# A decoder layer in fp32 on one core: a second pair of blocks by two levels, a longer preparation in the attention stages, and loads in another order

## The chip, the core and the metric

The kernel runs on one core of a Trainium2 chip. The core has engines that run their own instruction queues side by side: TensorE (PE in the profile; its weight loads are shown apart as PEld), VectorE (DVE), ScalarE (ACT), GpSimd (POOL) and SyncE (SP). DMA transfers are issued by an engine's queue and run beside all of them. The metric is the device time of one execution, in microseconds (us). Before the change it is 2240.34 us, the median of three runs (2240.03 to 2240.9).

## The reference

One decoder layer in fp32, for x of 16 batches x 128 rows x 1024 columns and a context of the same shape:

```python
x = x + attention(layernorm(x), Wqkv, bqkv, Wo, bo)       # one head of 256 columns
x = x + cross(layernorm(x), ctx, ctx, Wq, Wk, Wv, Wo, bo, g)
x = x + feed_forward(layernorm(x), gate, up, down)

def cross(q, k, v, Wq, Wk, Wv, Wo, bo, g):   # "linear" attention over 128 channels, 8 heads of 64
    qh, kh, vh = heads(q Wq), heads(k Wk), heads(v Wv)
    qh = softmax(qh, axis=head_dim) * SCALE
    kh = softmax(kh, axis=columns)
    context = einsum('bhdn,bhen->bhde', kh, vh)
    out = einsum('bhde,bhdn->bhen', context, qh) Wo + bo
    norm = maximum(sqrt(sum(out * out, axis=channels)), 1e-12)
    return out / norm * g * sqrt(128)

def feed_forward(x, gate, up, down):         # 1024 -> 2752 -> 1024
    Wg, Wu, Wd = dequantize(gate), dequantize(up), dequantize(down)
    # each: two int4 nibbles per int32, (nibble - zero) * scale in groups of 64
    return (silu(x Wg) * (x Wu)) Wd
```

## The kernel before

**Stages.** The program goes through five stages, one after the other:

1. Self-attention, four tiles of four batches (0 to 250 us of the profiled execution).
2. Cross-attention, one batch after the other (250 to 758 us). A batch takes four *key units* and four *query units*: a key unit is `kq <- wk_sb, cx` on TensorE, an exponential on ScalarE (`ek <- kq`, L727) and `kx <- ek, cxt` on TensorE; a query unit is `kq <- wq_sb, xn`, an exponential (`qe <- kq`, L795), a sum and reciprocal on VectorE, a multiplication on GpSimd (`qe`, L806), a transpose on VectorE, and a store and a load through DRAM (`kd`, then `qs`), after which `mm <- qs, m_sb` and the norm of the result follow, in `project_out`. The norm's root is Ln and Exp (L877, L878).
3. The gate and up projections of the feed-forward, pass 0: the tokens of batches 8 to 15 (758 to 1298 us).
4. The same, pass 1: the tokens of batches 0 to 7 (1298 to 1760 us).
5. The down projection (1760 to 2239 us).

**Multiplying by fewer products.** The 2752 rows of the feed-forward are cut into ten blocks of 256 and a last one of 192 (`RB = 10`). For a block by *one level*, a two by two split of weights and tokens is computed with seven products in place of eight (`one_block`; its products are the seven names of `GATE`). For a pair of blocks by *two levels* the seven are split once more, which makes 49 smaller products (`two_levels`, L1188 on: outer products `OUTERS`, in each of them seven inner ones). The combinations of inputs and results that this needs are made on VectorE and GpSimd: `ti` from the tokens, `li` from the weights, `C` and other sums from the results. Pass 1 works on all five pairs by two levels. In pass 0, `PAIRS = [3]` says which pairs are done so: blocks 6 and 7, the rest by one level, in the order 0 to 5, the pair, 8, 9, and the last block (`last_block`).

**Preparing the weights.** The weights are dequantised and combined for their seven products by `prepare` (a generator; each `next` is one *step*). A job is a block's matrix: "g", "u" or "d" (gate, up, down; "r" and "m" for the last block's gate and up). A job has two dequantising steps on VectorE (each two nibble operations and two multiplications or subtractions) and one step of four combinations; its seven results go to DRAM by seven stores of 256 KB. Raw weights are loaded on SyncE's queue, one or two units ahead. Before, `EARLY = 5` blocks' gate and up (ten jobs, thirty steps) are prepared in stage 1, with stores on GpSimd's queue, and the rest in stage 3, `rest`, with gate, up and down of each block in turn, and stores on SyncE's queue.

**What sets the order.** In stages 2 to 5 TensorE, VectorE and SyncE run in the program's order, through the wrappers `tensor`, `vector` and `sync` (class `InOrder`). All that goes through them is recorded at one line, L63, so the tiles' names tell it apart. The order of stage 2 is written out by hand: `later(n, fn)` puts `fn` into a list and `tick()`, called after each key unit and each query unit (eight ticks a batch), runs what has come due. At the end of stage 2 the ticks go on between the products of the first feed-forward block (`beside`), until the list is empty; `attention_done` then closes the pools of the cross-attention and opens those of the feed-forward. Self-attention's output projection for its last four batches (`give_half`, matmuls with `wo_again`) is queued so at the first ticks of the cross-attention.

**Loads at the stages' heads.** At the head of stage 2 SyncE's queue gets, in this order: `wk`, `wq`, `wv`, `xwo`, `xbo`, `gs`, then `cx` and `cxt` of the first two batches, then the two halves of `wo_again`. At the head of stage 3, four tiles of weights (`AHEAD = 4`) are loaded: the first on GpSimd's queue, the others on SyncE's; and the tokens' operands (`block_loads(0)`) come in eight loads on SyncE, two ticks apart. The loads of pass 1's tokens (`block_loads(1)`) are put beside every third product after the pair.

**The flag.** The softmaxes of the cross-attention are taken without subtracting the maximum (`plain`). `note` adds each sum and its reciprocal to two running totals on GpSimd (L659); at the end `raise_flag` compares these with `LIMIT` (1e18), counts the rows within it by a matmul with `ones` (`mm <- within`), and if any row is outside, a second copy of the whole program runs, with the maximum subtracted. In the executions here the second copy does not run. Before, one table of activation functions that has Ln and Exp both is loaded once ahead of the cross-attention (`preload_act_table_set`, L672).

Of the kernel before, what the change touches and what calls it, by code (L numbers as in the profile page):

```python
# [18 lines left out]
P = 128  # L19
# [47 lines left out]
def decoder_layer(  # L67
# [95 lines left out]
    def prep_pools(stack, name, c, ahead):  # L163
        for key, bufs in (("a", 3), ("c", c), ("raw", ahead + 1), ("sz", ahead + 1)):
            pools[key] = stack.enter_context(
                tc.tile_pool(name=f"{name}_{key}", bufs=bufs, side="right", reuse_waits="tile")
            )
# [4 lines left out]
    def load_raw(blk, mat, s):  # L172
# [3 lines left out]
        if mat == "d":  # L176
            raw, sz = raw[:w], pools["sz"].tile([P, 2, 512], F32, name="szd")[:w]
            nc.sync.dma_start(raw, dq[ds(start // 2, w), ts(s, 512)])
            for g in range(w // 32):
                row = dsz[start // GROUP + g, ts(s, 1024)].rearrange("(t f) -> t f", t=2)  # L180
                nc.sync.dma_start(sz[ts(g, 32)], row.partition_broadcast(32))
            return raw, *(sz[:, t].unsqueeze(1).to_broadcast([w, 2, 512]) for t in range(2))
# [12 lines left out]
        for m, off, w in parts:  # L195
            q, szs = matrices[m]
            nc.sync.dma_start(raw[:, :, ds(at, w)], q[:, :, ds(off, w)])
            nc.sync.dma_start(
# [6 lines left out]
    def prepare(jobs, ahead, queue, vector=nc.vector):  # L205
# [3 lines left out]
        loads = deque(load_raw(*u) for u in units[:ahead])  # L209
# [6 lines left out]
        for k, (blk, mat, s) in enumerate(units):  # L216
# [6 lines left out]
            if k + ahead < len(units):  # L223
                loads.append(load_raw(*units[k + ahead]))
# [61 lines left out]
    EARLY = 5  # L286

    def give_half(b, h, oT, wo_d, psum, tensor=nc.tensor, vector=nc.vector):
# [19 lines left out]
    prep_pools(first, "q", 4, 1)  # L308
    early = prepare(
        [(blk, mat) for blk in range(EARLY) for mat in "gu"], 1, nc.gpsimd, InOrder(tc, nc.vector)  # L310
    )
    give_pool = ExitStack()
    ag = give_pool.enter_context(tc.tile_pool(name="a_g", bufs=1, reuse_waits="tile"))
    with (
# [166 lines left out]
        for t in range(NT):  # L481
# [38 lines left out]
            else:  # L520

                for i in range(1, BPT):
                    give((t - 1) * BPT + i - 1, oT)
                    value(i, xnT, v)
                atT = turn_weights(at)
# [25 lines left out]
    def block_loads(p, blocks):  # L551

        for n, half in ((0, 0), (1, 0), (1, 1), (0, 1)):
            for i in range(2):
                src = xt_all[p][ds(half * BPT + 2 * i, 2), :, :, :, n]
                tc.keep_in_program_order(
                    nc.sync.dma_start(
# [44 lines left out]
    bcx = unit_pool("b_cx", 2)  # L602
    bw = unit_pool("b_w", 1)
    b0 = unit_pool("b_0", 2)
    bek = unit_pool("b_ek", 3)
    bas = unit_pool("b_as", 1)
    b3 = unit_pool("b_3", 3)
# [4 lines left out]
    bqs = side_pool("b_qs", 5)  # L612
    b1 = side_pool("b_1", 1)
    b2 = side_pool("b_2", 2)
    bps = side_pool("b_ps", 3, space=PSUM)

# [15 lines left out]
    if True:  # L632
        wq_sb = bw.tile([P, HIDDEN], F32, name="wq_sb")
# [7 lines left out]
        sync.dma_start(wk_sb, xwk)  # L641
        sync.dma_start(wq_sb, xwq)
        sync.dma_start(wv_sb, xwv.rearrange("(r p) s -> p r s", p=P))
        sync.dma_start(xwo_sb, xwo.rearrange("(r p) o -> p r o", p=P))
        sync.dma_start(xbo_sb, xbo)
        sync.dma_start(gs_sb, xg)
        vector.tensor_scalar(gs_sb, gs_sb, math.sqrt(S), None, ALU.mult)
        vector.memset(ones, 1.0)
        if plain:

            totals = [bs.tile([P, 2 * HEADS], F32, name=f"total{n}") for n in range(2)]
            for t in totals:
                nc.gpsimd.memset(t, 0.0)

        def note(*both):
            if plain:
                for t, v in zip(totals, both):
                    t = t[:, : v.shape[1]]
                    nc.gpsimd.tensor_tensor(t, t, v, ALU.add)  # L659

        def raise_flag():

            within = [small.tile([P, 1], F32, name=f"within{n}") for n in range(2)]
            for w, t in zip(within, totals):
                vector.tensor_reduce(w, t, AX.X, ALU.add)
                vector.tensor_scalar(w, w, LIMIT, None, ALU.is_le)
            vector.tensor_tensor(within[0], within[0], within[1], ALU.mult)
            ps = bps.tile([P, 1], F32, name="mm")
            tensor.matmul(ps, ones, within[0], start=True, stop=True)
            vector.tensor_copy(flag, ps[0:1])  # L670

        tc.keep_in_program_order(nc.scalar.preload_act_table_set("natural_log_exp_and_others"))  # L672
# [17 lines left out]
        def load_ctx(b):  # L690
            c = bcx.tile([P, C], F32, name="cx")
            sync.dma_start(c, cx[b])
            ct = bct.tile([P, NB, S], F32, name="cxt")
            sync.dma_start(ct, cxt[b])
            return c, ct

        def key_shift(c_sb):

            shift = bas.tile([P, 4, P], F32, name="kshift")
            for oc in range(4):  # L700
# [5 lines left out]
                nmax = small.tile([P, 1], F32, name="knmax")  # L706
# [4 lines left out]
        def key_unit(ctx, p, st):  # L711
# [17 lines left out]
            def use():  # L729
# [16 lines left out]
                if p == 3:  # L746
# [4 lines left out]
                    later(2, lambda: mix(st))  # L751
# [3 lines left out]
        def mix(st):  # L755
# [7 lines left out]
            ksum, krec = (small.tile([P, 4], F32, name=name) for name in ("ksum", "krec"))  # L763
            vector.tensor_copy(ksum, ks)
            vector.reciprocal(krec, ksum)
            note(ksum, krec)
# [17 lines left out]
        def query_unit(xn, pair, qs, wait):  # L784
# [3 lines left out]
            for i in range(2):  # L788
                tensor.matmul(
                    ps[:, i, :], xn[:, ts(2 * pair + i, P)], wq_sb, start=True, stop=True  # L790
# [5 lines left out]
            else:  # L796
                mx = small.tile([P, 2 * HEADS], F32, name="qmx")
# [4 lines left out]
            def weigh():  # L802
                den, rec = (small.tile([P, 2 * HEADS], F32, name=n) for n in ("qden", "qrec"))
# [3 lines left out]
                note(den, rec)  # L807
# [24 lines left out]
        def turned(b):  # L832
# [9 lines left out]
            if b == B - 1:  # L842
                blocks.update(new_blocks(xlate, lambda k: f"X{HB + 2 * k}"))
                loads = block_loads(0, blocks)
                for n in range(8):
                    later(7 + 2 * n, lambda: next(loads))
# [75 lines left out]


        batches = [p + i for p in PASSES for i in range(HB)]
        ctxs = {b: load_ctx(b) for b in batches[:2]}
        wo_again = []
        for d in range(2):
            wo_again.append(bqs.tile([P, C], F32, name="wo_again", tag="qs"))
# [972 lines left out]
```

## Time and profile before

The profiled execution took 2241.3 us; its span, from its first instruction to its last, is 2239.5 us. The table gives, for each stage of the profiled execution, its length, each engine's busy time in it, and the share of time in which the DMA engines were busy:

| stage (us of the span) | length | PE | DVE | ACT | POOL | DMA share |
|---|---|---|---|---|---|---|
| self-attention, 0 to 250 | 250 | 239.6 | 194.0 | 36.4 | 100.6 | 0.47 |
| cross-attention, 250 to 758 | 508 | 502.1 | 339.5 | 243.4 | 208.4 | 0.62 |
| its end, 758 to 850 (with block 0) | 92 | 86.7 | 53.7 | 31.4 | 15.2 | 0.73 |
| pass 0, blocks to 5, 850 to 1074 | 224 | 222.1 | 151.3 | 27.9 | 6.3 | 0.82 |
| pass 0, blocks 6 and 7 by two levels, 1074 to 1163 | 89 | 85.7 | 75.0 | 15.7 | 35.2 | 0.50 |
| pass 0, blocks 8 and 9, 1163 to 1260 | 97 | 97.0 | 61.9 | 12.8 | 0.0 | 0.97 |
| pass 0, last block, 1260 to 1298 | 38 | 38.0 | 23.5 | 4.7 | 6.5 | 0.55 |
| pass 1, all pairs by two levels, 1298 to 1722 | 424 | 423.3 | 323.8 | 82.7 | 181.0 | 0.49 |
| pass 1, last block, 1722 to 1760 | 38 | 38.0 | 17.1 | 5.3 | 0.0 | 0.95 |
| down projection, 1760 to 2239 | 479 | 472.0 | 242.6 | 8.7 | 0.0 | 0.48 |

The page's slices, 56 us each, show the granted TensorE clock and each engine's share, in tenths:

```profile
PE   8999899999999999999999999999999999999998
DVE  6997466667667657666796658787787645544462
ACT  2111135454554431111111112121121000000000
PEclk9999999999999999999999999999999999999999
```

How to read it: PE near its whole length in every stage means that TensorE has work nearly all the time. A wait of TensorE shows as a difference between length and PE. The other engines have room in every stage, though not the same room.

### The profile page before, as it was taken

The page shows a single profiled execution, that of the slowest core. Times are in us where ns is not written, and L with a number is a line of the kernel's source. Part 1 is how long each engine was busy: PE and PEld are TensorE (multiplying, and loading weights), DVE is VectorE, ACT ScalarE, POOL GpSimd, SP SyncE. Part 2 cuts the span into 40 slices and gives each one's busy share as a digit, 9 for nine tenths or more (in the row PEclk, how much of TensorE's full clock was granted, in tenths as well). Part 3 has the DMA queues.
Part 4 walks back from the last instruction along what each step waited for, and adds up shares of the span by engine and source line. Part 5 has one row for each costly group of instructions (what it writes and reads, how often), then busy time and mean ns, then how long its engine had stood idle before and what let it go on. Part 6 is the DMA issues. An engine that isn't in the chain of part 4 may idle for free.

```text
span 2239.5 us, 24114 instructions
## 1 busy us (share of the span) xinstructions
PE 2204.4 (98%) x8330; PEld 1517.3 (68%) x8330; DVE 1482.2 (66%) x2055; ACT 468.9 (21%) x651; POOL 553.1 (25%) x543
## 2 busy tenths in 40 slices
PE   8999899999999999999999999999999999999998
PEld 7556555555555544444774488888887688888887
DVE  6997466667667657666796658787787645544462
ACT  2111135454554431111111112121121000000000
POOL 5452044444444400001320044444442000000000
PEclk9999999999999999999999999999999999999999
DMA  6435246666686768887649834454554964333731
GB/s 251 157 130 169 85 132 198 209 205 197 208 258 192 225 182 287 284 267 253 199 166 301 251 100 158 167 197 155 175 198 165 350 211 164 114 125 129 226 118 39
DMA packets 270835, 425.23 MB, mean 190 GB/s; under 512 B 28784, under 2 KB 130544, under 8 KB 270576
## 3 DMA queue, kind: packets, MB, share of 16 engines
q1 hardware_dynamic: 244624, 377.72, 52.5%
q0 software_dynamic: 8064, 27.27, 3.3%
q10 hardware_dynamic: 18016, 18.62, 2.7%
q8 instruction: 68, 1.11, 0.2%
q14 instruction: 63, 0.52, 0.1%
HBM read 265.62 MB, written 157.35 MB: 189 GB/s over the span
## 4 chain that ended last, share of the span: by engine, by line
PE 90%; DVE 6%; issue 2%; DMA 1%; POOL 1%; ACT 0%; SPq 0%; DVEq 0%; POOLq 0%; ACTq 0%
PE po L1780 21%; PE q L63 20%; PE p L63 18%; PE kq L63 9%; PE mm L63 8%; PE kx L63 5%; PE mm L396 4%; PE mm L411 2%; DVE pa L63 2%; PE p L1157 1%; PE mm L292 1%; PE tr L343 1%; DVE ti L63 1%; DMA wo_again<-in_wo 0%; POOL qe L806 0%
## 5 line engine op out<-in xcount | busy, mean ns | idle before, releaser
L63 PE MATMUL p<-b,w 128*128 128x512 f32 x560 | 248.2, 596 | 1.9 <-DVE sg L63 1.9
L63 PE MATMUL q<-ti,li 128*128 128x256 f32 x1008 | 232.2, 379 | 3.5 <-DVE ti L63 2.8
L63 POOL TENSOR_TENSOR li<-w 128x512 f32<-128x512 f32 x84 | 118.1, 1408 | 433.3 <-DMA w<-wu 244.8
L63 PEld LDWEIGHTS q<-ti,li 128*128 128x128 f32 x1008 | 191.0, 190 | 31.3 <-issue 2.8
L63 PEld LDWEIGHTS p<-b,w 128*128 128x128 f32 x560 | 106.9, 191 | 136.4 <-issue 128.8
L1780 PE MATMUL po<-wc,lc 128*128 128x256 f32 x840 | 183.4, 379 | 0.0
L63 PE MATMUL p<-T,w 128*128 128x512 f32 x400 | 177.2, 592 | 0.0
L1780 PEld LDWEIGHTS po<-wc,lc 128*128 128x128 f32 x840 | 159.6, 190 | 21.8
L63 ACT COPY k<-q 128x512 f32<-128x512 f32 x126 | 73.7, 585 | 399.2 <-PE q L63 399.2
L63 PEld LDWEIGHTS p<-T,w 128*128 128x128 f32 x400 | 76.0, 190 | 95.7 <-issue 95.2
L1780 PE MATMUL po<-wq,lq 128*128 128x256 f32 x560 | 126.7, 379 | 0.2 <-issue 0.2
L806 POOL TENSOR_TENSOR qe<-qe,qrec 128x1024 f32<-128x1024 f32 x64 | 122.0, 1906 | 11.5 <-DVE qrec L63 9.3
L63 PEld LDWEIGHTS mm<-qs,m_sb 128*128 128x128 f32 x512 | 97.3, 190 | 40.1 <-issue 26.8
L63 PE MATMUL kq<-wk_sb,cx 128*128 128x512 f32 x256 | 120.4, 592 | 2.5 <-DMA cx<-in_cx 2.5
L63 PE MATMUL kx<-ek,cxt 128*128 128x512 f32 x256 | 121.8, 598 | 0.0
L63 PE MATMUL mm<-qs,m_sb 128*128 128x256 f32 x512 | 120.8, 379 | 0.0
L63 PE MATMUL kq<-wq_sb,xn 128*128 128x512 f32 x256 | 120.3, 593 | 0.0
L1780 PEld LDWEIGHTS po<-wq,lq 128*128 128x128 f32 x560 | 106.0, 190 | 15.8 <-issue 0.8
L63 DVE TENSOR_TENSOR pa<-pa,sz 128x1024 f32<-128x1024 int32 x86 | 112.6, 1309 | 2.5
L396 PE MATMUL mm<-xnT,wqkv_sb 128*128 128x512 f32 (+1 forms) x320 | 112.9, 509 | 0.0
L63 DVE STREAM_TRANSPOSE kt<-qe 128x1024 f32<-128x1024 f32 x64 | 79.5, 1242 | 43.7 <-POOL qe L806 43.5
L727 ACT ACTIVATE ek<-kq 128x1024 f32<-128x1024 f32 x64 | 65.3, 1020 | 147.4 <-PE kq L63 147.4
(201 smaller groups left out, 3595.7 us busy)
## 6 DMA issues: line engine op xcount, KB each, us to landing
w<-wu SPq DMA_DIRECT2D x140, 256.0 KB, 3.6
lq<-h SPq DMA_DIRECT2D x140, 256.0 KB, 4.4
w<-wg SPq DMA_DIRECT2D x138, 256.0 KB, 2.8
kd<-kt SPq DMA_DIRECT2D x64, 512.0 KB, 2.9
qs<-kd SPq DMA_DIRECT2D x256, 128.0 KB, 3.2
h<-hc SPq DMA_DIRECT2D x80, 256.0 KB, 2.8
wq<-wd SPq DMA_DIRECT2D x70, 256.0 KB, 5.3
h<-h SPq DMA_DIRECT2D x60, 256.0 KB, 3.0
```

Source lines behind the costliest of these rows:

```text
L63: return lambda *args, **kw: self._tc.keep_in_program_order(fn(*args, **kw))
L292: tensor.matmul(ps, oT[:, d, ts(b % BPT, S)], wo_d[d][:, ts(h, 512)], start=(d == 0), stop=(d == 1),)
L343: nc.tensor.transpose(tr[:, j, :], xn[:, ts(4 * h + j, P)], ident)
L396: nc.tensor.matmul(ps[:, tokens], wqkv_sb[:, f, c, :], xnT[:, c, tokens], start=(c == 0), stop=(c == CC - 1),)
L411: nc.tensor.matmul(ps, xnT[:, c, ts(i, S)], wqkv_sb[:, 4:6, c, :], start=(c == 0), stop=(c == CC - 1),)
L727: nc.scalar.activation(ek, ps, AF.Exp)
L806: nc.gpsimd.tensor_tensor(qe, qe, rec.unsqueeze(2).to_broadcast(wide), ALU.mult)
L1157: tensor.matmul(ps, wt[:, j, :], T[q][:, :, j], start=(first == q and j == 0), stop=(q in (2, 3, 4) and j == JC - 1), skip_group_check=True,)
L1780: nc.tensor.matmul(bank[:, i, :], l[:, ts(i, S)], w,  start=(start and c == 0 and i % 2 == 0), stop=(stop and c == len(pairs) - 1), skip_g ...
```

## The change

- **Pairs.** `PAIRS = [3, 4]`: in pass 0 blocks 8 and 9 are also done by two levels, right after blocks 6 and 7. `ti` gets a third buffer, and the operands for the outer product after q = 7 are made beside the second outer product before it. The operands of the last block (`outer_operand`) are made at other products of it.
- **Preparation.** One list `todo` holds all jobs: gate and up of blocks 0 to 9, then "r" and "m", then all "d". Stage 1 does 11 jobs (`EARLY`), three steps more than before, one after each value unit of its last tile. The three next (`MIDDLE = 14`), nine steps, are done in the cross-attention, one at the fifth tick of each of nine batches, with raw loads on `sync` and stores on GpSimd's queue. In block 0 `rest` has a step at the last product alone; its steps per product change in `beside`, and `attention_done` first runs what is left of `middle`. `pools["a"]` has 3 buffers before, 2 or 3 now; `pools["c"]` 4.
- **Head of the cross-attention.** SyncE's queue now gets `wk`, `cx` and `cxt` of the first batch, `wo_again`, then `wq`, `wv`, `xwo`, `xbo`, `gs`, then the second batch. `mix_weights` comes four ticks later, `give_half` two ticks later; the pools are made in another order, and small tiles get a pool of their own (`bsm`).
- **The flag.** `note` and its totals are gone. The sums themselves are kept in a tile of 1088 columns, whose maximum and minimum `raise_flag` takes at the end; the counting matmul comes four ticks after. The load of the activation table ahead of the cross-attention is gone too.
- **Feed-forward's head and pass 1's tokens.** All four first weight tiles go on GpSimd's queue; `block_loads(0)` goes on ScalarE's queue, three ticks apart; `block_loads(1)` is issued all at once after the two-level stage.
- **Ticks.** `mix` two ticks later; `project_out` one tick later for batches up to the thirteenth; the operand for q = 5 one batch later.

The diff, cut to its core:

```diff
+    todo = [(blk, mat) for blk in range(RB) for mat in "gu"] + [(RB, "r"), (RB, "m")]
+    todo += [(blk, "d") for blk in range(len(BLOCKS))]
+    EARLY, MIDDLE = 11, 14
...
-    prep_pools(first, "q", 4, 1)
-    early = prepare(
-        [(blk, mat) for blk in range(EARLY) for mat in "gu"], 1, nc.gpsimd, InOrder(tc, nc.vector)
-    )
+    prep_pools(first, "q", 3, 1)
+    early = prepare(todo[:EARLY], 1, nc.gpsimd, InOrder(tc, nc.vector))
...
                     value(i, xnT, v)
+                    next(early, None)
...
+    prep_pools(sides, "x", 2, 1)
+    middle = prepare(todo[EARLY:MIDDLE], 1, nc.gpsimd, vector, sync)
...
+        batches = [p + i for p in PASSES for i in range(HB)]
+        nc.sync.dma_start(wk_sb, xwk)
+        ctxs = {batches[0]: load_ctx(batches[0])}
+        wo_again = []
+        for d in range(2):
+            wo_again.append(bqs.tile([P, C], F32, name="wo_again", tag="qs"))
+            nc.sync.dma_start(wo_again[d], wo[ts(d, P)])
+        nc.sync.dma_start(wq_sb, xwq)
...
+        ctxs[batches[1]] = load_ctx(batches[1])
...
+            sums = bs.tile([P, B * 4 * 2 * HEADS + B * 4], F32, name="sums")
...
-                vector.tensor_reduce(w, t, AX.X, ALU.add)
-                vector.tensor_scalar(w, w, LIMIT, None, ALU.is_le)
+                vector.tensor_reduce(w, sums, AX.X, op)
+                vector.tensor_scalar(w, w, limit, None, test)
...
+            later(4, count)
...
-        tc.keep_in_program_order(nc.scalar.preload_act_table_set("natural_log_exp_and_others"))
...
-                    later(2, lambda: mix(st))
+                    later(4, lambda: mix(st))
...
-            note(ksum, krec)
...
-                note(den, rec)
...
-                loads = block_loads(0, blocks)
+                loads = block_loads(0, blocks, nc.scalar)
                 for n in range(8):
-                    later(7 + 2 * n, lambda: next(loads))
+                    later(4 + 3 * n, lambda: next(loads))
...
-                when = (13, 14, 15, 16, 17, 1, 1)
+                when = (14, 15, 16, 17, 18, 1, 1) if k < 13 else (13, 14, 15, 16, 17, 1, 1)
...
+            for n in (5,) if k < 9 else ():
+                later(n, lambda: next(middle, None))
...
-        PAIRS = [3]
+        PAIRS = [3, 4]
...
-                            bufs=1 if self.kept else 2,
+                            bufs=1 if self.kept else 3,
...
-                if not last:
+                if not last and not (ps == 0 and q == 7):
                     right.extend(operands.inner_right(OUTERS[n + 1][1]))
+                if ps == 0 and q == 3:
+                    extra.extend(operands.inner_right(OUTERS[n + 2][1]))
...
-            load_weights(nc.gpsimd if n == 0 else nc.sync)
+            load_weights(nc.gpsimd)
...
                 if blk == 0:
-                    steps = 1
+                    steps = n == 13
                 elif blk == RB:
-                    steps = n in (0, 2, 4)
+                    steps = n < 4
                 else:
-                    steps = (1, 1 + (mat == "g" and blk < 3), 1, 0, 1, 0, 0)[n % 7]
+                    steps = (1, 1 + (mat == "g"), 1, 0, 1, 0, 0)[n % 7]
...
-                pass1_loads = block_loads(1, pass1)
+                for _ in block_loads(1, pass1):
+                    pass
```

## The prediction

> **What bounds the kernel now.** I read the page's busy row first, then what TensorE waited for, the chain that ended last in order of time, the granted clock around each wait, and ScalarE's and VectorE's timelines. Times are of the profiled execution: span 2239.5 us, run 2241.3 us, 1.0 us above the median of the three runs (2240.34); my sum is taken off both alike.
>
> ```profile
> PE 2204.4 (98%) x8330; PEld 1517.3 (68%) x8330; DVE 1482.2 (66%) x2055; ACT 468.9 (21%) x651; POOL 553.1 (25%) x543
> ```
>
> TensorE is busy 98% of the span, so a microsecond is gained only by fewer matmuls or by a TensorE wait that goes. Its waits:
>
> ```profile
> PE p L1157 <- DMA w<-wg: 4.9, 1, 4.9
> PE q L63 <- DVE ti L63: 3.3, 4, 2.4
> PE mm L63 <- DMA wo_again<-in_wo: 3.1, 1, 3.1
> PE kq L63 <- DMA cx<-in_cx: 2.5, 1, 2.5
> PE p L63 <- DVE sg L63: 1.9, 1, 1.9
> PE mm L63 <- DVE within L63: 0.6, 1, 0.6
> ```
>
> Left out are the start (9.4 us for x) and waits below 0.9 us. A wait costs more than itself, for TensorE comes back at a lower clock. Three stretches right after a wait (columns: stretch, length, then each engine's busy time, granted clock, DMA share, GB/s):
>
> ```profile
> 259.69:263.19 3.50, 3.50 (x4) 1.47 (x5) 0.00 (x0) 0.00 (x0) 0.00 (x0) 0.51 0.03 9
> 762.71:768.99 6.28, 6.28 (x9) 2.69 (x10) 4.81 (x10) 0.00 (x0) 3.85 (x7) 0.56 1.04 358
> 852.94:865.04 12.10, 12.10 (x24) 5.26 (x25) 10.75 (x16) 2.33 (x5) 0.00 (x0) 0.86 0.98 332
> ```
>
> At 0.43 us a 128x512 matmul (next fence) these would take 1.72, 3.43 and 10.3 us: 1.8, 2.85 and 1.8 us more are lost.
>
> **Two levels for blocks 8 and 9.** Row prices are start to start:
>
> ```profile
> 1071.04 3.60 PE L63 MATMUL p<-b,w 128*128 128x512 f32 x8
> 1074.48 1.89 PE L63 MATMUL q<-b,w 128*128 128x256 f32 x8
> 1076.20 3.62 PE L63 MATMUL q<-ti,li 128*128 128x256 f32 x16
> ```
>
> A one-level matmul is (1074.48 - 1071.04)/8 = 0.430 us, a two-level one (1076.20 - 1074.48)/8 = 0.2155 us. Two blocks hold 2 x 14 products x 4 chunks, each fp32 matmul two instructions: 224. As a pair they hold 7 x 7 products x 4, again doubled: 392. So 96.3 us go and 84.5 us come: **-11.8 us**. Bounds: the pair at before's own pace (1074.48 to 1163.42, 88.9 us, waits in) gives -7.4; nothing gives more than -11.8.
>
> The waits in that stage (3.3 us) are VectorE's `ti`: 2.44 us ahead of the last outer product, because the widest outer (q=7) also had the next `ti` to make; 0.9 us behind dequantising steps (4.38 us at 1114.70). The third `ti` buffer and the operand made from q=3 on remove the first; the 0.9 comes twice. 3.3 becomes 1.8: **-1.5 us**, between -3.3 (none left) and +3.3 (before's waits twice). VectorE is busy 85.1 of the 104 us from 1060 to 1164.
>
> **Loads at the cross-attention's head.** Before, SyncE issues wk at 244.73, when the last value matmul frees wqkv; cx is seventh (247.80), `wo_again` last (249.84, 10 us to land). Phase one's matmuls end at 250.4. After, in the built order, both cxt and wk precede cx; wk's room is that of a bias, free earlier; cx takes wqkv's room and issues near 244.7, `wo_again` by 246.5. At the 4 MB in 15 us (244.7 to 259.7, 267 GB/s) seen here, cxt, cxt, wk, cx and `wo_again` (2.75 MB) are in by about 255 even if all begin at 244.7. The first key unit may want cx at 250.4, the first `wo_again` matmul now comes after four units (257.3). 0.2 + 2.5 + 3.1 + 1.8 = 7.6 us go; I take **-7.0**, between -7.6 and -3 (cx as late as 6.8 us after issue, one slow restart).
>
> **The feed-forward's head** costs 4.9 + 2.85 + 0.6 + 1.9 + 1.8 = 12.1 us now. After:
> - The first weight loads stand on GpSimd's queue behind the same multiply (759.7). That multiply loses the bookkeeping op before it (1.29 us at 756.43) and a group of about 1 us on VectorE; the T operand moved one batch later (2.28 us) may give that back. Load there at 760.3 to 762.6, TensorE there at 757.8 + 1.9 (next point): wait about 1.5, restart 1.5.
> - The last three query units now stand without a matmul between. The last needs a bank that ScalarE frees only after two table loads, two Ln and an Exp (4.8 us): 1.9.
> - The flag: two maxima over 1088 columns at 1.2 us (row of the 128x1024 reduce) and three small ops are 2.9 us where 0.8 stands. Last norm matmul to flag was 811.1 to 823.0, so 14 us; TensorE has three products of 3.43 us in front of its matmul. Wait 3.8, restart 1.5. The order puts that matmul ahead of blk 1's second product, so all of TensorE queues behind it.
> - A one-column bank wait behind the added Silu/Ln switching: about 1.
> Together 11.2: **-1 us**, between -7 (only the flag's wait is real) and +5 (each 1.5 us longer).
>
> **Parts I cost at nothing.** *Table loads.* Without the preload the built order holds 28 more table loads: Ln, then Exp again, in 14 batches, 1.28 us each, 35.9 us on ScalarE. Rows of such loads, and the batch as it is:
>
> ```profile
> 786.04 1.28 ACT L877 ACT_TABLE_LOAD   x1
> 787.33 1.08 ACT L877 ACTIVATE sq<-mm 128x512 f32<-128x512 f32 x2
> 788.44 1.28 ACT L878 ACT_TABLE_LOAD   x1
> 789.73 1.06 ACT L878 ACTIVATE sq<-sq 128x1024 f32<-128x1024 f32 x1
> ...
> 469.62 1.02 ACT L795 ACTIVATE qe<-kq 128x1024 f32<-128x1024 f32 x1
> 475.06 1.02 ACT L727 ACTIVATE ek<-kq 128x1024 f32<-128x1024 f32 x1 [4.42 <-PE kq L63]
> ```
>
> Cover: one batch is 31.2 us, of TensorE work alone. Count from the norm matmul (0). ScalarE ends `qe` at 1.2, loads, Ln, Ln, loads, Exp: 6.0; `ek` 7.0; `qe` 8.1. TensorE wants that `ek` at 8.8 and the banks at 10.5 and 12.2. **Slack 1.8 us**; cover gone, 2.6 us x 14 = 36 us. What queues behind `ek` is the kx matmul and with it TensorE.
> The Trainium skill ("ScalarE: Activation LUTs", What ACT_TABLE_LOAD costs) speaks against this edit: 1283 ns plus a 1380 ns drain for each switch. The rows show 0.01 to 0.03 us between a load and its neighbours, no drain. By the page two drains make `ek` end at 9.8, 1.0 us late, 14 times: the sum would be 13 us worse.
>
> *Nine steps in the cross-attention:* six of 0.76 + 2.48 us and three of four 0.69 us combinations, one a batch. VectorE's batch goes from 21.5 to 24.7 of 31.2 us; counted as above it is through its list at 2.7 and then waits for Exp at 6.0, so 3.3 us of cover; gone, 9 x 3.2 = 29 us. Their 12 loads stand on SyncE in front of a kd store whose consumer stands a tick (3.9 us) further off than before; their 21 stores (0.6 us each) stand on GpSimd, which loses 160 bookkeeping ops (0.2 us, at times 1.2). *Three steps at phase one's end* (9.2 us on VectorE, idle about half of 200 to 250): the attention copy ends at 246.5, wanted at 248.4. *Pass-one block loads all at once:* eight 512 KB loads from about 4 us after the two-level stage, at 267 GB/s in by 20 us; their operand is wanted at 20.5 by VectorE's count and by TensorE after the last block's 38 us. One to two us either way over these four; I take 0.
>
> **Sum:** -11.8 - 1.5 - 7.0 - 1.0 = -21.3 us: 2241.3 becomes 2220.0, the median **2219.0 us**.
>
> **The rivals.**
> - *The saving is paid back where it is made.* VectorE at 82% in the two-level stage becomes the bound, GpSimd's `li` (42% in pass one) slowing it, and the second pair takes the 96 us that two blocks took. For: VectorE ops there swell from 0.69 to 1.75 us beside GpSimd. Against: pass one runs five such pairs with TensorE at 100%. Loses 13.3 us: 2232. Chance 0.22, with the feed-forward head at its worst.
> - *ScalarE takes the chain (slower).* Place: the `ek` behind the second table load in each of 14 batches. From 1.8 us of extra delay on TensorE waits; from 1.8 + 21.3/14 = 3.3 us the gain is gone. At 2.5 us of wait a batch, 35 us: 2254. For: 28 loads in the FIFO that frees the banks, and only 0.2 us between `sq` and the norm matmul. Against: ScalarE at 58% of a batch. Chance 0.11.
> - *Nothing measurable:* both half true, 2236 to 2245. Chance 0.05.
>
> **How the numbers follow.** Forecast 0.62, its own range 2208 to 2227 (bounds of the head terms). I stretch to 2234 for the first rival and leave the slower one out. 0.2% (4.5 us) is about what a measurement can tell from no change: faster 0.62 + 0.22 = 0.84, same 0.05, slower 0.11.
>
> **What would show it.** Matmuls 8330 give or take to about 8498 (-224 + 392); the two-level stage of pass zero 169 to 173 us long; no wait for cx or `wo_again`; 28 more table loads in the batches with TensorE still at 100% and a batch of 31.2 us; a wait for `within` of 3 to 5 us. Wrong if a batch lengthens past 31.5 us, or if the two-level stage shows `ti` or `C` waits above 5 us.

## The result, and the profile after

The changed kernel takes 2250.26 us (median of five runs, 2249.59 to 2252.74), the kernel before 2240.9 us in the same comparison (five runs, 2240.03 to 2242.9): slower by a ratio of 1.0045, 95% interval 1.003 to 1.0059. The profiled execution has a span of 2248.5 us, 9.0 us longer than before's.

The page's busy row of the changed kernel (each engine's busy time, its share of the span, instructions):

```profile
PE 2195.5 (98%) x8498; PEld 1549.3 (69%) x8498; DVE 1565.4 (70%) x2120; ACT 509.6 (23%) x685; POOL 566.6 (25%) x443
```

TensorE runs 8498 matmuls, 168 more, as the change of blocks 8 and 9 says, and is busy 8.9 us less. It stands still 18 us more. Its waits (who waited for whom: total, times, longest):

```profile
PE p L1161 <- DVE h L63: 11.2, 1, 11.2
...
PE mm L63 <- DMA qs<-kd: 9.0, 5, 3.1
PE q L63 <- DVE ti L63: 6.1, 5, 2.4
PE p L1161 <- DMA w<-wg: 2.8, 1, 2.8
PE kq L63 <- ACT qe L808: 1.6, 1, 1.6
PE q L63 <- ACT k L63: 1.5, 2, 0.7
PE p L63 <- DVE h L63: 1.0, 1, 1.0
```

Left out is the start. The waits for cx, `wo_again`, `sg` and `within` are gone. Two large new ones, for `h` at the feed-forward's head and for `qs` in the cross-attention, take 20.2 us. Where the 9.0 us came from, by the starts of TensorE's rows in the two profiles (the last column is e5_both, the fastest version found, below):

| stretch | before | after | difference | e5_both |
|---|---|---|---|---|
| start to the wait for the first weight tile | 757.8 | 763.4 | +5.6 | 751.3 |
| from there to the two-level stage | 316.7 | 323.3 | +6.6 | 310.3 |
| blocks 6 to 9 | 185.1 | 179.5 | -5.6 | 178.0 |
| last block of pass 0 | 37.8 | 39.1 | +1.3 | 39.3 |
| pass 1 | 462.5 | 462.5 | 0 | 462.6 |
| down projection and end | 479.7 | 480.7 | +1.0 | 480.4 |

### The profile page after: what moved, and what is told of

Its sections match the earlier page's. It is cut to its first block, busy times and chain, and to the rows that moved or that the text cites. A ratio compares the mean times of both kernels' runs of the same rounds, so it can differ in the third digit from the quotient of the medians.

```text
span 2248.5 us, 24452 instructions
## 1 busy us (share of the span) xinstructions
PE 2195.5 (98%) x8498; PEld 1549.3 (69%) x8498; DVE 1565.4 (70%) x2120; ACT 509.6 (23%) x685; POOL 566.6 (25%) x443
## 4 chain that ended last, share of the span: by engine, by line
PE 87%; DVE 7%; DMA 2%; issue 2%; ACT 1%; POOL 1%; SPq 0%; DVEq 0%; ACTq 0%; POOLq 0%
PE q L63 23%; PE po L1787 21%; PE p L63 13%; PE kq L63 9%; PE mm L63 7%; PE kx L63 5%; PE mm L397 4%; PE p L1161 2%; PE mm L412 2%; DVE pa L63 1%; PE mm L295 1%; DMA b<-xt 1%; DVE ti L63 1%; DVE C L63 1%; PE tr L344 1%
## 5 line engine op out<-in xcount | busy, mean ns | idle before, releaser
L63 PE MATMUL q<-ti,li 128*128 128x256 f32 x1176 | 272.2, 381 | 7.0 <-DVE ti L63 5.5
L63 PEld LDWEIGHTS q<-ti,li 128*128 128x128 f32 x1176 | 223.2, 190 | 40.2 <-POOL li L63 8.8
L63 POOL TENSOR_TENSOR li<-w 128x512 f32<-128x512 f32 x98 | 140.7, 1437 | 333.1 <-DMA w<-wu 239.0
L820 POOL TENSOR_TENSOR qe<-qe,qrec 128x1024 f32<-128x1024 f32 x64 | 148.1, 2313 | 197.4 <-DVE qrec L63 170.4
L63 ACT COPY k<-q 128x512 f32<-128x512 f32 x147 | 86.0, 585 | 468.5 <-PE q L63 468.5
L63 PE MATMUL p<-b,w 128*128 128x512 f32 x432 | 190.5, 593 | 1.0 <-DVE h L63 1.0
L1787 PE MATMUL po<-wc,lc 128*128 128x256 f32 x840 | 183.4, 379 | 0.0
L1787 PEld LDWEIGHTS po<-wc,lc 128*128 128x128 f32 x840 | 159.6, 190 | 21.8
L63 PEld LDWEIGHTS p<-b,w 128*128 128x128 f32 x432 | 81.9, 190 | 103.4 <-issue 99.0
L63 PE MATMUL p<-T,w 128*128 128x512 f32 x304 | 134.7, 592 | 0.0
L1787 PE MATMUL po<-wq,lq 128*128 128x256 f32 x560 | 126.7, 379 | 0.1
L1787 PEld LDWEIGHTS po<-wq,lq 128*128 128x128 f32 x560 | 106.0, 190 | 15.7 <-issue 1.0
L63 POOL TENSOR_TENSOR li<-w,li 128x512 f32<-128x512 f32 x49 | 67.8, 1384 | 186.6 <-PE q L63 166.3
L63 PEld LDWEIGHTS p<-T,w 128*128 128x128 f32 x304 | 57.8, 190 | 72.7 <-issue 72.5
```

The source lines that it names most:

```text
L63: return lambda *args, **kw: self._tc.keep_in_program_order(fn(*args, **kw))
L820: nc.gpsimd.tensor_tensor(qe, qe, rec.unsqueeze(2).to_broadcast(wide), ALU.mult)
L1787: nc.tensor.matmul(bank[:, i, :], l[:, ts(i, S)], w,  start=(start and c == 0 and i % 2 == 0), stop=(stop and c == len(pairs) - 1), skip_g ...
```

## Where the two new waits come from, in the trace

**qs.** Between 570 and 612 us the waits of SyncE's queue show one entry that before has not, and the timeline shows it happen. SPq and ACTq are the queues in which SyncE and ScalarE issue their transfers. Columns of the timeline: start, length, engine, line, operation, transfers.

```profile
SPq L63 <- DMA b<-xt: 21.4, 2, 13.1
```

```profile
580.64 0.30 SPq L63 DMA_DIRECT2D xt<-kt  x1
...
590.19 0.39 ACTq L559 DMA_DIRECT2D b<-xt  x1
...
594.09 1.27 SPq L63 DMA_DIRECT2D xt<-kt  x3
```

SyncE issues the first of four stores `xt<-kt`. The other three stand still for 13.1 us, until a load `b<-xt` has landed that ScalarE issues at 590.19, behind the Ln and Exp of a batch. These stores have no need of that load. In the built program the transfers of SyncE and ScalarE share eight completion marks, handed out in turn while the program is built, and a transfer waits for the one that held its mark before (the four stores as they stand in it):

```
L63 DMACopy xt0_1551<-kt_3593 32x4x256 [waits DVE_49]
L63 DMACopy xt0_1551<-kt_3593 32x4x256 [waits DMAHW7_49]
L63 DMACopy xt0_1551<-kt_3593 32x4x256 [waits DMAHW0_49]
L63 DMACopy xt0_1551<-kt_3593 32x4x256 [waits DMAHW1_49]
```

In that order the transfer that held mark DMAHW7 before the second store is the first of the eight `b<-xt` loads. A load put on ScalarE's queue is thus waited for on SyncE's, by whatever comes next on its mark; cx, `qs` and `kd` queue up behind it.

**h.** VectorE's and TensorE's timelines of the changed kernel at the feed-forward's head (in brackets: idle time before, and what ended it):

```profile
825.44 3.60 PE L1161 MATMUL p<-T,w 128*128 128x512 f32 x8
840.24 6.05 PE L1161 MATMUL p<-b,w 128*128 128x512 f32 x8 [11.20 <-DVE h L63]
```

```profile
803.88 1.25 DVE L63 STREAM_TRANSPOSE kt<-xn 128x1024 f32<-128x1024 f32 x1 [1.04 <-ACT xn L152]
828.64 1.23 DVE L63 SCALAR_TENSOR_TENSOR y<-sq,y 128x1024 f32<-128x1024 f32 x1 [23.52 <-ACT sq L891]
...
836.57 1.25 DVE L63 TENSOR_REDUCE within<-sums 128x1 f32<-128x1088 f32 x1
...
837.92 1.28 DVE L63 TENSOR_REDUCE within<-sums 128x1 f32<-128x1088 f32 x1
...
839.50 0.69 DVE L63 TENSOR_TENSOR h<-p,k 128x512 f32<-128x512 f32 x1
```

VectorE works in program order. `y` of the last batch is next from 805 on and needs that batch's norm; every `h`, which frees a bank (the room in which a product's sums are kept) for block 0's products, stands behind it. The last norm matmul in before, then in the changed kernel:

```profile
810.25 1.02 PE L63 MATMUL mm<-sq,ones 128*128 128x512 f32 x2
```

```profile
824.48 1.12 PE L63 MATMUL mm<-sq,ones 128*128 128x512 f32 x2 [0.50 <-ACT sq L882]
```

In before it ends at 811.1 and there are 42 executed matmuls of block 0 left to lie over VectorE's chain; here it ends at 825.4 and 16 are left. The two maxima of the flag stand in the chain ahead of the `h` that ends the wait; with their small operations they take 2.9 us of it (836.57 to 839.50). From the cross-attention to the end of pass 1, block 0's matmuls are the only ones that aren't held to the program's order (`engine = nc.tensor if blk == 0`; the down projection's matmuls, L1787, aren't either), so the builder, the software that turns the kernel into the engines' instruction lists, places them by its own expectation. In the built order, of block 0's 56 matmul instructions (each executed twice) so many stand ahead of the last norm matmul:

```
before            35
after             48
e2_ahead          35   (after, three of the first four weight tiles on SyncE again)
e12_before_ahead  48   (before, all four on GpSimd)
```

With any one of these undone instead (the operand loads' queue, the table preload, `mix`, the ticks of `project_out`, the T operand) the count in the built order stays 48.

## The experiments

**e1_queue: the operand loads back on SyncE's queue.**

```diff
-                loads = block_loads(0, blocks, nc.scalar)
+                loads = block_loads(0, blocks, nc.sync)
```

> The changed kernel with one edit: the eight operand loads b<-xt go on SyncE's queue again, at the same ticks as in the changed kernel. Theory: between 575 and 700 us SyncE's stores and loads (xt<-kt, qs<-kd) stand still until a b<-xt load that waits in ScalarE's queue has landed (21.4 us of SyncE waits, 13.1 the longest), which makes TensorE wait 9.0 us for qs. On SyncE's own queue those waits go: waits for qs below 1 us, 9 to 11 us less, about 2240. Rival A: the nine preparation steps or the load rate make qs late, and the waits stay at about 9 us, 2250. Rival B: the loads on SyncE cost it as much as they save, 2248 or more.

2239.21 us (ratio to before 0.999, 0.9981 to 0.9999), 11.0 us less than the changed kernel. No wait for qs is left. TensorE reaches the wait for the first weight tile at 751.2 us in place of 763.4. Between 570 and 720 us SyncE waits for b as little as this (in the changed kernel 42.6 us from 560 to 720):

```profile
SPq L63 <- DMA b<-xt: 0.7, 1, 0.7
```

Rivals A and B fall.

**e2_ahead: three of the first four weight tiles on SyncE's queue.**

```diff
-            load_weights(nc.gpsimd)
+            load_weights(nc.gpsimd if n == 0 else nc.sync)
```

> The changed kernel with one edit: of the first four weight tiles of the feed-forward only the first is on GpSimd's queue, three on SyncE's, as before the change. Block 0's matmuls are not held to the program's order; in the built order 35 of its 56 then stand ahead of the last batch's norm matmul, as before the change, where the changed kernel has 48. Each runs as two of 0.43 us, so the norm comes 11.2 us earlier and leaves 11.2 us more of products to lie over VectorE's chain behind it. Theory: the wait of 11.2 us for h falls to 0 to 2 us, 2238 to 2240. Rival: the two maxima over 1088 columns make the chain late by themselves (my step on the flag: a wait of 3.8 us stays), 2243; or the wait stays above 8 us, 2249.

2236.06 us (0.9977, 0.9968 to 0.9986), 14.2 us less. The wait of 11.2 us and the slow restart behind it (a row of 6.05 us instead of 3.60) make 13.7 us of it. The row that waited in the changed kernel, at 840.24, now stands without a wait:

```profile
828.80 3.70 PE L1161 MATMUL p<-b,w 128*128 128x512 f32 x8
```

The two maxima are still there and cost nothing, for the products now lie over them.

**e3_preload: the activation table with Ln and Exp loaded ahead again.**

```diff
+        tc.keep_in_program_order(nc.scalar.preload_act_table_set("natural_log_exp_and_others"))
```

> The changed kernel with the load of the activation table that has Ln and Exp put back ahead of the cross-attention. It takes 28 table loads of 1.28 us from ScalarE, two a batch. Theory: they lie in ScalarE's slack, and the time is that of the changed kernel within 2 us, 2249 to 2252; 28 fewer ACT_TABLE_LOAD in the profile. Rival (my slower case, ScalarE takes the chain): 10 us or more less, below 2241.

2250.74 us, the changed kernel's time. ScalarE has 28 instructions fewer and 34.3 us less to do, and nothing comes of it:

```profile
PE 2197.2 (98%) x8498; PEld 1552.5 (69%) x8498; DVE 1553.6 (69%) x2120; ACT 475.3 (21%) x657; POOL 572.8 (25%) x443
```

The wait for the Exp of the last query unit (1.6 us) went, and that for the first weight tile grew from 2.8 to 4.7 us: TensorE comes to it 2.0 us earlier and starts on it at 766.06 us, in place of 766.18. The loads thus cost nothing in this kernel, where the tile sets the time at that place.

**e4_steps126: one dequantising step moved within the two-level stage.**

```diff
-                    0, PAIRS, first_operands, lambda q: q in (1, 6, 5) and next(rest, None)
+                    0, PAIRS, first_operands, lambda q: q in (1, 2, 6) and next(rest, None)
```

> The changed kernel with one edit in pass 0's two-level stage: the dequantising step after the outer product q=5 is done after q=2. Theory: VectorE makes two sets of ti in q=3, and the step of 4.6 us ahead of it leaves it late, so TensorE waits 2.4 us for ti in each pair; without the step the waits for ti in this stage fall from 5.5 us to below 2 us, and the time by 3 to 5 us, to about 2246. Rival: two sets of ti in one outer product are too much by themselves, the 2.4 us stay, 2250.

2251.93 us (2249.46 to 2254.42): no gain. The outer products come in the order q = 1, 2, 6, 5, 3, 7, 4, and the steps in a fixed order of their own: dequantising, combinations, dequantising. So the edit moves two steps, the combinations from behind q=6 to behind q=2, and the second dequantising step from behind q=5 to behind q=6. The wait at q=3 did go, but one as long came in both pairs behind the combinations, in the first pair 10 us after their end at 1121.3:

```profile
1131.57 1.97 PE L63 MATMUL q<-ti,li 128*128 128x256 f32 x8 [2.31 <-DVE ti L63]
...
1221.46 1.97 PE L63 MATMUL q<-ti,li 128*128 128x256 f32 x8 [2.31 <-DVE ti L63]
```

**e8_before_act: before, with the operand loads on ScalarE's queue.** The edit of e1_queue turned round, with the changed kernel's ticks (`later(4 + 3 * n, ...)`).

> The kernel before with one edit, the converse of e1_queue: the eight operand loads b<-xt go on ScalarE's queue, three ticks apart, as in the changed kernel. Theory: SyncE's xt<-kt and qs<-kd stand behind a b<-xt that waits in ScalarE's queue, so waits for qs of 7 to 10 us appear between 570 and 700 us that before has not, 2250. Rival: the waits need the later ticks or the fuller VectorE of the changed kernel, no change, 2241.

2247.41 us (1.0025, 1.0016 to 1.0034): 6.4 us slower, two thirds of what I expected, and the wait for qs is 2.9 us, not 7 to 10. The cause is there, in SyncE's waits (first line, 560 to 720 us) and TensorE's (second):

```profile
SPq L63 <- DMA b<-xt: 31.8, 5, 9.9
```

```profile
PE mm L63 <- DMA qs<-kd: 2.9, 1, 2.9
```

So the changed kernel's steps aren't needed for it. The loss lies ahead of the first weight tile, which TensorE reaches 6.3 us later than in before. Of it 2.9 us are this wait, 1.5 us the eight matmuls behind it (a row of 3.40 us for 1.89), 0.7 us a wait for `qrec` just ahead of it; the rest isn't placed.

**e5_both: e1_queue and e2_ahead together.**

> The changed kernel with the edits of e1_queue and e2_ahead together: operand loads b<-xt on SyncE's queue, three of the first four weight tiles on SyncE's queue. Theory: the two losses are at different places and add up: 11 us and 14 us off 2250.5 give 2225 to 2226, with neither the wait of 11.2 us for h nor the waits for qs. Rival: they share a cause, and together they give little more than one, 2234 to 2237.

2223.6 us (0.9922, 0.9909 to 0.9936): 26.7 us less than the changed kernel, 17.5 us less than before. The two add up (11.0 and 14.2 us alone). Its waits, without the start:

```profile
PE q L63 <- DVE ti L63: 5.5, 4, 2.4
PE p L1161 <- DMA w<-wg: 2.8, 1, 2.8
PE q L63 <- ACT k L63: 2.1, 3, 0.7
PE kq L63 <- ACT qe L808: 1.6, 1, 1.6
PE p L63 <- DVE h L63: 1.3, 1, 1.3
```

**e9_pool: the operand loads on GpSimd's queue, else e5_both.**

```diff
-                loads = block_loads(0, blocks, nc.scalar)
+                loads = block_loads(0, blocks, nc.gpsimd)
```

> e5_both with one difference: the eight operand loads b<-xt are on GpSimd's queue, neither on ScalarE's nor on SyncE's. In the built kernel SyncE's stores wait for marks that SyncE's and ScalarE's transfers take in turn, and GpSimd's transfers take marks of their own. Theory (shared marks): SyncE doesn't wait for b<-xt, no waits for qs, 2223 to 2226. Rival (any queue other than SyncE's, or the loads themselves, holds SyncE up): waits for qs of 7 to 9 us as in e2_ahead, 2234 to 2236.

2223.56 us, no wait for qs, and SyncE doesn't wait for b. So it isn't a foreign queue as such, nor the loads; it is the pairing of ScalarE's queue with SyncE's.

**e12_before_ahead: before, with all four first weight tiles on GpSimd's queue.** The edit of e2_ahead turned round.

> The kernel before with one edit, the converse of e2_ahead: all four first weight tiles of the feed-forward on GpSimd's queue. The built order then has 48 of block 0's 56 matmuls ahead of the last batch's norm matmul where before has 35. Theory: the norm and VectorE's chain behind it come 11 us later, TensorE waits 8 to 11 us for h or the flag, 2249 to 2252. Rival: the late chain is the work of the new flag or of the later ticks, no change, 2241.

2253.59 us (1.0055, 1.0041 to 1.0069): 12.4 us slower from one line. TensorE waits at the flag's matmul, which needs the end of the same chain:

```profile
PE mm L63 <- DVE within L63: 8.4, 1, 8.4
```

The rival falls: neither the new flag nor the later ticks are needed.

**e7_pairs3: e5_both without the second pair.**

```diff
-        PAIRS = [3, 4]
+        PAIRS = [3]
```

> e5_both with PAIRS = [3], so that blocks 8 and 9 are done by one level again. It prices the second pair alone. My step (11.8 us of matmuls and 1.5 us of waits): 12 to 13 us slower than e5_both, about 2238. By the lengths of the stages in the profiles of before and after (185.2 and 179.5 us for blocks 6 to 9): 6 us slower, about 2231. Rival (VectorE bound, the pair takes what two blocks took): the time of e5_both, 2225.

2237.78 us, 14.2 us slower than e5_both. That fits my number, but for a wrong reason. Blocks 8 and 9 by one level took 104.8 us in its profile where before needs 96.1, because of a wait that only this version has:

```profile
PE p L63 <- DVE sg L63: 5.5, 1, 5.5
```

The 24 matmuls behind it take 13.46 us where such a row takes 10.46. Against blocks at before's pace the second pair takes 89.0 us (half of 178.0), so it is worth 7.1 us.

**e6_extra5: the operands after q=7 made beside q=5.** Moved from q=3 to q=5, with the step as in e4_steps126.

```diff
-                if ps == 0 and q == 3:
-                    extra.extend(operands.inner_right(OUTERS[n + 2][1]))
+                if ps == 0 and q == 5:
+                    extra.extend(operands.inner_right(OUTERS[n + 3][1]))
```

> e5_both with two edits in pass 0's two-level stage: the operands for the outer product after q=7 are made beside q=5 and not beside q=3, and the dequantising step after q=5 is done after q=2. Theory: the waits for ti come from making two sets of ti in one outer product that also finishes its sums (q=3); in q=5 there is room once the step is gone. Waits for ti fall from 5.5 us to below 1.5 us, 4 to 6 us less than e5_both, about 2221. Rival: the extra set is too much wherever it is put, and the waits stay at 4 us or more, 2225.

2226.77 us, 3.2 us slower: the waits for ti grew to 8.1 us in the stage (four, 2.9 the longest). The rival holds.

**e11_noextra: e5_both without making them early.**

```diff
-                if not last and not (ps == 0 and q == 7):
+                if not last:
...
-                if ps == 0 and q == 3:
-                    extra.extend(operands.inner_right(OUTERS[n + 2][1]))
```

> e5_both without making the operands after q=7 early (they are made beside q=7 again); the third ti buffer stays. My step said that making them early takes away 2.4 us of waits a pair. If so: 4 to 6 us slower than e5_both, 2228 to 2230. By the profiles of before (3.3 us of waits a pair) and of e5_both (3.5 us a pair) the wait is only moved from q=7 to q=3: the time of e5_both within 2 us.

2226.88 us, 3.3 us slower than e5_both, with wide runs (2222.71 to 2228.54; the profiled one is the slowest); the waits for ti are 6.4 us for 5.5 us. The long waits are back at q=7, 3.4 and 2.4 us for 2.4 and 2.4, and blocks 6 to 9 take 183.1 us for 178.0. That is more than the waits differ by; the rest is a slow restart, which e5_both's waits of 2.4 us didn't have:

```profile
1142.45 3.75 PE L63 MATMUL q<-ti,li 128*128 128x256 f32 x8 [3.38 <-DVE ti L63]
1146.00 3.16 PE L63 MATMUL q<-T,w 128*128 128x256 f32 x8
```

```profile
1234.30 3.44 PE L63 MATMUL q<-ti,li 128*128 128x256 f32 x8 [2.44 <-DVE ti L63]
```

These three rows are 4.7 us longer than at full clock (1.89 each). The time lies between the two expectations: making the operands early moves the wait and takes 0.9 us off it; how much of the other 2.4 us it brings in every run, these runs don't show.

**e10_nosteps: e5_both without preparation steps in the two-level stage.**

```diff
-                two_levels(
-                    0, PAIRS, first_operands, lambda q: q in (1, 6, 5) and next(rest, None)
-                )
+                two_levels(0, PAIRS, first_operands)
...
-                    steps = (1, 1 + (mat == "g"), 1, 0, 1, 0, 0)[n % 7]
+                    steps = (1, 2, 1, 0, 1, 0, 0)[n % 7]
```

> e5_both with no preparation steps in pass 0's two-level stage; the five or six steps are done beside blocks 1 to 5, one more for each up matrix. Theory: the waits for ti and k (7.0 us in this stage) are VectorE's load, 3.2 us of steps an outer product among it, and fall to 3 us or less: 4 to 6 us less than e5_both, 2218 to 2220. Rival: they come from the order in which ti and the sums are made inside one outer product, as e6_extra5 suggests, and stay above 4 us: 2222 to 2225.

2235.93 us, 12.3 us slower than e5_both. Yet in the stage itself the theory held: no wait for ti is left, 1.2 us for k, and blocks 6 to 9 take 172.6 us for 178.0. The loss is beside it. TensorE's waits from 1030 to 1300 us, and VectorE's rows at the two places:

```profile
PE p L63 <- DVE h L63: 14.4, 2, 8.7
```

```profile
1053.35 2.92 DVE L63 TENSOR_SCALAR pa<-raw 128x512 int32<-128x512 int32 x2 [6.15 <-issue]
...
1273.97 0.76 DVE L63 TENSOR_SCALAR pa<-raw 96x512 int32<-96x512 int32 x2 [6.70 <-DMA wd<-pa]
```

One step beside block 5 stood still for 6.15 us before it wrote `pa`, one beside the last block 6.70 us until a store of `pa` had left (1.44 us in e5_both), and VectorE's `h`, behind them in the order, kept TensorE's banks. For the second the release is named; for the first the profile names none.

## Why the prediction was wrong, step by step

I said 2219 us, faster; it was 2250.26 us, slower.

- **The loads on ScalarE's queue: no term at all.** The step that failed first is one that isn't there. I costed the block loads of pass 1 and left out those of pass 0, though the change moves them onto another queue, and of the queues that I did cost I asked only what stands in them. It costs 11.0 us (e1_queue), and 6.4 us in before (e8_before_act); it is what makes the table's first row 5.6 us longer in place of 6.5 us shorter.
- **The feed-forward's head: -1.0 us forecast, +6.6 us and 1.6 us of the bank wait in the row above it found.** The wait for the weights (1.5 forecast, 2.8 found) and for the bank (1.9, 1.6) were of the right kind and near. The flag's step failed at its cover. The chain from the norm was near what I'd said (14.8 us, from 825.4 to the end of `h` at 840.2, for 14), but I counted on three products, 10.3 us, over it, from before's trace; one was left, 3.4 us. The change of one queue had the builder place 13 more matmul instructions, 26 executed, 11.2 us, ahead of that norm. The wait was 11.2 us in place of 3.8, and for `h`, not for `within`. With the old placing the maxima cost nothing (e2_ahead); with the new one before loses 12.4 us without them (e12_before_ahead).
- **Two levels for blocks 8 and 9: -11.8 - 1.5 forecast, -5.6 found (-7.1 in e5_both).** The 168 matmuls were right (the price of a small one is 0.215 us, not 0.2155, which is 0.2 us in the sum). The sign of the waits was wrong: I let 3.3 us become 1.8; they became 7.0, beyond my upper bound of twice 3.3 and past my own sign of being wrong (5 us). The third `ti` buffer and the early operands moved the long wait from q=7 to q=3, they didn't remove it:

```profile
1154.72 2.88 PE L63 MATMUL q<-ti,li 128*128 128x256 f32 x8 [2.43 <-DVE ti L63]
...
1245.24 1.97 PE L63 MATMUL q<-ti,li 128*128 128x256 f32 x8 [2.42 <-DVE ti L63]
```

  What makes it is VectorE's load at that place. In the first pair VectorE's rows show no pause from 1116 to 1158 us; a dequantising step of 4.6 us stands in them at 1139.77, and the `ti` that TensorE wants ends 10 us behind the step. The wait moves when the steps move (e4_steps126), and without steps there is none, at q=3 or at q=7 (e10_nosteps). So making the operands early did answer before's wait; the sum missed that q=3 has no room for a second set beside a step. A step alone doesn't make a wait for `ti`: those behind q=1 and q=6 leave none. The 1.5 us between -5.6 and -7.1 come of a slow restart behind the first of these waits (rows of 2.88 and 2.70 us for 1.89), which e5_both didn't have. So the first rival, VectorE as the bound in this stage, was half true: the pair gave the lower of my two bounds (-7.4), not nothing.
- **The cross-attention's head: -7.0 forecast, right.** e5_both, with neither new wait, reaches the first weight tile 6.5 us before before does, with the new bank wait of 1.6 us in it: about 8.1 us gained, some 0.6 of it at the end of the first stage.
- **Table loads, nine steps, three steps: nothing forecast, right.** e3_preload prices the loads at nothing. In the batches that take the nine steps, VectorE is fuller and TensorE doesn't notice (before, then the changed kernel; length, then PE, PEld, DVE, ACT, POOL, clock, DMA share, GB/s):

```profile
500.00:550.00 50.00, 50.00 (x180) 28.53 (x179) 35.39 (x48) 25.59 (x30) 21.79 (x26) 1.00 0.61 188
```

```profile
500.00:550.00 50.00, 50.00 (x165) 28.42 (x164) 43.16 (x55) 26.90 (x31) 19.74 (x15) 1.00 0.71 222
```

  The second rival, ScalarE takes the chain, falls with e3_preload: the kernel was slower, but not by that. The Trainium skill ("ScalarE: Activation LUTs", What ACT_TABLE_LOAD costs) adds a drain of 1380 ns to each load; with it I had worked out 13 us of loss, and the measured difference is 0.5 us in the other direction, inside the spread of the runs.
- **The last block: +1.3 us, not foreseen.** TensorE waits 1.0 us for `h` behind the operands of pass 1 that the change put between its last products.

With the two missed losses undone, e5_both takes 2223.6 us, inside the range I gave and 4.6 us above the forecast. That is partly luck, for terms cancel. By the profiles it gains 17.7 us for 21.3: the two levels bring 6.2 us less than forecast, the last block and the rest behind it cost 2.3 us, while the feed-forward's head gains 4.8 us for 1.0, and the cross-attention's head 1.1 us more. The range itself doesn't follow from what I said of it: the bounds of the two head terms give 2212 to 2229 us, not 2208 to 2227.

## What to carry to other kernels

When a transfer moves to another engine's queue, ask not only what stands in that queue but who waits for the transfer: completion marks can be shared between queues, and then a load that is late in one holds up another that has nothing to do with it. Where a builder places work that is not held to an order, one edit elsewhere moves that work; count in the built order what stands ahead of the instruction that the end hangs on, and don't carry a cover over from the old trace. And a wait that moves when a step is moved is a matter of that engine's load at that place; taking the step out removes the wait there, but the step has to go somewhere, and here it cost more at the new place (e10_nosteps).

## What the hardware showed that I had not expected

How much a wait of TensorE costs beyond itself varies for waits of nearly one length. Four of the changed kernel's (eight 128x256 matmuls take 1.72 us start to start at full clock; their rows show 1.89):

```profile
609.12 1.96 PE L63 MATMUL mm<-qs,m_sb 128*128 128x256 f32 x8 [1.86 <-DMA qs<-kd]
...
650.18 3.49 PE L63 MATMUL mm<-qs,m_sb 128*128 128x256 f32 x8 [3.08 <-DMA qs<-kd]
```

In the row behind 1.86 us of waiting the granted clock was 1.00, behind 3.08 us it was 0.54, and behind 2.4 us (the two rows shown under the two-level stage) once 0.67 and once 1.00. The wait of 2.8 us for the first weight tile was followed by eight matmuls in 5.37 us here (0.67) and in 6.64 us in e5_both (0.54), where 3.60 is the row at full clock. The Trainium skill ("TensorE: Matmul & The Clock Gate", Part 1: The HAM clock gate) says that the clock falls to half after an idle window of about 3.4 us, and that the window runs freely, which it gives as the reason why the point of change varies. The spread agrees with a free window; that a lower clock is seen after 2.4 us of waiting is earlier than the figure.
